# A band and time attention block: the feed-forward transposes behind the second product, the output products half a step later, the band scores of four heads in turn, a reciprocal on VectorE at the change to gelu

## The chip, the cores and the metric

The kernel runs on one core of one Trainium2 chip. The core has TensorE (PE, the matrix engine, with its weight loads shown apart as PEld), VectorE (DVE), ScalarE (ACT), GpSimd (POOL) and a queue for transfers (SP). Each engine executes its own instructions in order, and semaphores tie the engines together. The metric is the time of one execution in device microseconds (us); several runs are taken, and their median counts. A profile of one execution gives each instruction's start and duration.

## The reference

The input x has shape (2, 256, 128, 128): batch, time, band, channel. Three blocks follow each other, each added to x:

```python
xt = _ln(x, ln_t_w, ln_t_b).transpose(0, 2, 1, 3)
x = x + _mha(xt, t_wi, t_bi, t_wo, t_bo, H_T, cm).transpose(0, 2, 1, 3)
xf = _ln(x, ln_f_w, ln_f_b)
x = x + _mha(xf, f_wi, f_bi, f_wo, f_bo, H_F, bm)
xn = _ln(x, ln_n_w, ln_n_b)
h = jax.nn.gelu(xn @ w1.T + b1, approximate=False)
x = x + (h @ w2.T + b2)
```

The first attends over the 256 times of one band with a causal mask, the second over the 128 bands of one time with a mask that keeps bands at most 16 apart. Both have four heads of 32 channels; the softmax is over the keys. The third has 512 hidden channels. All of it is float32.

## The kernel before

**Groups.** `BoundedPath.groups` (L824) cuts the work into groups of four rows of 128 tokens. There are 128 groups of attention over time (`OverTime`, L599), whose results go to a buffer in HBM. Then come 32 batches of sixteen times each: a batch has four groups of attention over bands (`OverBands`, L673), called A0 to A3 here, and four groups of feed-forward (`FeedForward`, L736), called F0 to F3, that work on what A0 to A3 left in the tile `x2`. F0 needs what A0 wrote, F1 what A1 wrote, and so on.

**Order.** Every instruction of PE, DVE, ACT and POOL goes through `InOrder` (L786), which pins it in the order in which the program writes it. That order is written out by hand in `run` (L876). Its loop takes one step n for each group; in step n it issues pieces of several groups: `do(n, ...)` is a piece of group n, `do(n - 1, ...)` one of the group before. `near(n, far, name)` issues a preparing piece for a group further on, which is group n + 2 + far for attention and n + 1 + far for feed-forward (`AHEAD`, L430 and L737). So each engine has a queue that is fixed beforehand, and an instruction that waits holds up all that stand behind it on its engine.

**The pieces of a group of attention.**

- `statistics` (L444): mean and variance of four rows on DVE (bn_stats, bn_aggr), then 1/sqrt on POOL in two instructions (the tile `rstd`). `normalize` (L456): four instructions on DVE (`xh`). `transpose` (L465): four transposes on PE into one bank (`xp`). `take_transposed` (L472): a copy on DVE (`xnT`).
- `queries_keys`, `values`: the products `qp`, `kp`, `vp` on PE; their copies to SBUF (`qT`, `kT`, `v`) run on ACT, for time groups `kT` on DVE.
- `scores`: the products `sp`, keys by queries, one head in one quarter of PE's rows (32 of 128), each head in a bank of its own. `weights`: the exponentials on ACT (tiles `pt` for time, `pf` for bands), then the mask: selects on POOL, two for each band head, and for the fourth band head one multiplication with a 0/1 band on DVE. Band groups did heads 0 and 1 in `first_half` and `first_function`, heads 2 and 3 in `second_half` and `second_function`.
- `bias`: on POOL, the residual plus a constant row.
- `weigh`: the denominators `rp` (products with ones) and the weighted values `op`. `invert` (L563): on ACT the logarithm of `rp` and the exponential of its negative, a first estimate `r` of the reciprocal. `divide` (L571): on DVE one Newton step and the division, `t`, `u` and `oT`.
- `output` (L581): four products `yp` on PE. `finish` (L589): on DVE, `yp` added to the residual; time groups then issue two stores.

**The pieces of a feed-forward group.** `statistics` to `take_transposed` as above. `hidden` and `gelus`: four products `hp` on PE and four gelus `hT` on ACT, two in the first half, two in the second. `weigh`: the second product `zp`, 16 products. `divide`: on DVE, `zp` added to the residual `res`, and a store.

Each product in float32 appears as two instructions in the trace. All results of PE go through one set of eight PSUM banks (L807), which the tiles take in turn. ACT needs one table for exp and ln and another for gelu, so it changes its table twice in each batch: `preload_act_table_set` (L898) ahead of A0, and by itself ahead of F0's first gelu. In the step of F0 (`turn`) the exponentials of A3's reciprocal stand ahead of F0's gelus, so that the table changes after them.

Of the kernel before, what the change touches and what calls it, by code (L numbers as in the profile page):

```python
# [9 lines left out]
F32 = mybir.dt.float32  # L10
# [3 lines left out]
ALU = mybir.AluOpType  # L14
# [4 lines left out]
P = 128  # L19
H = 4  # L20
# [4 lines left out]
NT = 4  # L25
# [4 lines left out]
EXP_SET = "natural_log_exp_and_others"  # L30
# [393 lines left out]
class Group:  # L424
# [52 lines left out]
    def first_half(self):  # L477
        pass

    def first_function(self):  # L480
        pass

    def second_half(self):
        pass

    def second_function(self):
        pass
# [25 lines left out]
    def output(self):  # L513
        pass
# [5 lines left out]
class Attention(Group):  # L520
# [50 lines left out]
    def divide(self):  # L571
# [6 lines left out]
        self.oT = path.work.tile([P, NT * P], F32, name="oT", bufs=2)  # L578
        vector.scalar_tensor_tensor(self.oT, t, 2.0, u, ALU.subtract, ALU.mult)

    def output(self):  # L581
        path = self.path
        self.yp = path.bank([P, NT, P], "yp")
        for i in range(NT):
            path.tensor.matmul(
                self.yp[:, i], self.oT[:, i * P : (i + 1) * P], path.k.wn[self.which], start=True, stop=True
            )
# [85 lines left out]
class OverBands(Attention):  # L673
# [32 lines left out]

    def first_half(self):
        self.p = self.path.work.tile([P, H, NT, P], F32, name="pf", tag="p")
        self.scores((0, 1))

    def first_function(self):
        self.weights((0, 1))

    def second_half(self):
        self.scores((2, 3))

    def second_function(self):
        self.weights((2, 3))

    def weigh(self):  # L720
        path = self.path
# [79 lines left out]
class BoundedPath:  # L801
# [74 lines left out]
    def run(self, x, out):  # L876
        groups = list(self.groups(x, out))

        def do(n, *names):
            if 0 <= n < len(groups):  # L880
                for name in names:
                    getattr(groups[n], name)()

        def near(n, far, name):

            for d in (1, 2):
                if 0 <= n + d + far < len(groups) and groups[n + d + far].AHEAD == d:
                    do(n + d + far, name)

        def at(n, kind):  # L890
            return 0 <= n < len(groups) and isinstance(groups[n], kind)

        self.scalar.preload_act_table_set(EXP_SET)
        for n in range(-7, len(groups) + 2):

            turn = at(n, FeedForward) and at(n - 1, OverBands)
            if at(n, OverBands) and at(n - 1, FeedForward):
                self.scalar.preload_act_table_set(EXP_SET)  # L898
            do(n + 7, "load")
            near(n, 1, "statistics")  # L900
            near(n, 0, "normalize")
            do(n, "first_half")
            if not turn:
                do(n, "first_function")
            do(n, "bias")
            do(n - 1, "weigh", "invert", "divide")
            if turn:
                do(n, "first_function")
            do(n, "second_half", "second_function")
            do(n + 1, "queries_keys", "take_query", "take_key", "values", "take_values")  # L910
            near(n, 0, "transpose")
            near(n, 0, "take_transposed")
            do(n - 1, "output", "finish")


def bounded_path(tc, k, x, out):
# [66 lines left out]
```

## Time and profile before

| what | value |
|---|---|
| median of 3 runs | 3305.75 us (3305.04 to 3305.8) |
| profiled execution, its own time | 3304.75 us |
| its span | 3302.9 us |
| granted clock of TensorE | 0.999 |
| PE busy | 3183.9 us (96%) |
| DVE busy | 2191.5 us (66%) |
| POOL busy | 1843.4 us (56%) |
| ACT busy | 1803.8 us (55%) |
| stretch 100 to 1000 us (time groups): PE busy | 900 of 900 us |
| stretch 1600 to 3000 us (batches): PE busy | 1338.5 of 1400 us |

Busy time is the time in which an engine executes at least one instruction. The ends of PE's instructions are modelled, and its instructions overlap, so its busy share is not the share of its peak; what a piece costs is better read as the distance from its start to the start of what follows. The list of groups gives, for one kind of instruction, its count, its busy time, its mean duration in ns, and the idle time of its engine just before it with what ended that time. The view of waits sums that idle time by who waited for whom: total, number, longest.

### The profile page before, as it was taken

Reading aid. Unit: us, or ns where it says so; the run is one execution under the profiler, and the core shown is the slowest. Engines: PE = TensorE matmul, PEld = TensorE weight load, DVE = VectorE, ACT = ScalarE, POOL = GpSimd, SP = SyncE. Lnnn points to the kernel's source line nnn. Section 1 sums busy time; section 2 is a strip of 40 time slices with the busy share of each in tenths; the row PEclk is TensorE's granted clock in tenths of the full one; section 3 lists DMA queues with packets and bytes.
Section 4 is the critical chain, followed back from the end, with each engine's and each line's share of the span. In section 5 each row is a group of like instructions: output and inputs, shape, how many; then the busy total and the mean of one; then the engine's idle time right before and its main releaser. Section 6 shows DMA issues by size and latency. Waiting matters only on the chain.

```text
span 3302.9 us, 77870 instructions
## 1 busy us (share of the span) xinstructions
PE 3183.9 (96%) x31270; PEld 2259.0 (68%) x31270; DVE 2191.5 (66%) x6446; ACT 1803.8 (55%) x3264; POOL 1843.4 (56%) x2441
## 2 busy tenths in 40 slices
PE   7999999999999999999999999999999999999998
PEld 5666666666666766676667666676667666677666
DVE  6777777777777766566665666566665666566664
ACT  4666666666666654555445544555445545455544
POOL 4555555555555655456555565455555565455554
PEclk9999999999999999999999999999999999999999
DMA  3222222222222111110111011110111011110000
GB/s 80 59 70 57 72 56 59 72 56 72 56 59 72 52 40 30 33 30 27 39 33 33 27 39 30 33 30 27 39 33 33 27 37 32 33 30 27 27 20 21
DMA packets 222866, 140.57 MB, mean 43 GB/s; under 512 B 7968, under 2 KB 205984, under 8 KB 222496
## 3 DMA queue, kind: packets, MB, share of 16 engines
q1 hardware_dynamic: 221248, 134.45, 14.5%
q8 instruction: 249, 4.08, 0.5%
q10 hardware_dynamic: 1248, 1.05, 0.1%
q14 instruction: 121, 0.99, 0.1%
HBM read 68.36 MB, written 67.11 MB: 41 GB/s over the span
## 4 chain that ended last, share of the span: by engine, by line
PE 89%; DVE 7%; ACT 2%; issue 1%; DMA 0%; POOL 0%; SPq 0%; ACTq 0%; DVEq 0%
PE sp L796 14%; PE zp L796 14%; PE hp L796 12%; PE rp L796 10%; PE qp L796 8%; PE vp L796 7%; PE op L796 7%; PE kp L796 7%; PE yp L796 6%; PE xp L796 4%; DVE xnT L796 2%; DVE oT L796 1%; DVE t L796 1%; ACT r L796 1%; DVE u L796 1%; ACT ln L796 1%
## 5 line engine op out<-in xcount | busy, mean ns | idle before, releaser
L796 POOL TENSOR_SCALAR rstd<-mv 128x4 f32<-128x4 f32 x384 | 88.1, 229 | 1225.5 <-DVE mv L796 1223.8
L796 ACT ACTIVATE hT<-hp,b 128x512 f32<-128x512 f32 x512 | 341.3, 687 | 514.4 <-PE hp L796 510.6
L796 POOL TENSOR_SCALAR_AFFINE_SELECT pf<-pf 128x512 f32<-128x512 f32 x768 | 545.3, 718 | 100.3 <-ACT pf L796 74.1
L796 ACT ACTIVATE pt<-sp 128x384 f32<-128x384 f32 x1024 | 419.3, 496 | 303.5 <-PE sp L796 303.5
L796 PE MATMUL hp<-xnT,w1f 128*128 128x512 f32 x1024 | 493.9, 605 | 52.9 <-DVE xnT L796 52.9
L796 PE MATMUL sp<-qT,kT 32*128 32x128 f32 (+1 forms) x8192 | 536.2, 315 | 0.0
L796 PEld LDWEIGHTS zp<-w2T_sb,hT 128*128 128x128 f32 x4096 | 475.0, 192 | 50.4 <-issue 46.4
L796 PEld LDWEIGHTS sp<-qT,kT 32*128 32x128 f32 x8192 | 433.2, 185 | 87.6 <-issue 55.1
L796 DVE COPY xnT<-xp 128x512 f32<-128x512 f32 x384 | 261.8, 689 | 333.2 <-PE xp L796 332.0
L796 PE MATMUL zp<-w2T_sb,hT 128*128 128x128 f32 x4096 | 481.5, 276 | 0.1
L796 ACT ACTIVATE pf<-sp 128x512 f32<-128x512 f32 x512 | 277.9, 595 | 306.1 <-PE sp L796 282.9
L796 POOL TENSOR_TENSOR rstd<-rstd,mhalf 128x4 f32<-128x4 f32 x384 | 405.0, 1055 | 32.0
L796 DVE TENSOR_TENSOR t<-rp,r 128x512 f32<-128x512 f32 x256 | 177.0, 692 | 314.3 <-ACT r L796 311.8
L796 PEld LDWEIGHTS vp<-wf,xnT 128*128 128x128 f32 x2048 | 269.7, 192 | 123.0 <-issue 92.2
L796 POOL TENSOR_SCALAR_AFFINE_SELECT pt<-pt 128x512 f32<-128x512 f32 x512 | 314.0, 637 | 58.5 <-ACT pt L796 58.4
L796 PE MATMUL yp<-wn,oT 128*128 128x128 f32 x2048 | 275.1, 277 | 43.1 <-DVE oT L796 43.1
L796 PEld LDWEIGHTS hp<-xnT,w1f 128*128 128x128 f32 x1024 | 174.2, 190 | 202.0 <-issue 131.3
L796 PEld LDWEIGHTS yp<-wn,oT 128*128 128x128 f32 x2048 | 248.6, 192 | 56.4 <-PE xp L796 56.4
L796 PE MATMUL qp<-xnT,wf 128*128 128x512 f32 x512 | 285.8, 640 | 0.8 <-DVE xnT L796 0.8
L796 DVE SCALAR_TENSOR_TENSOR oT<-t,u 128x512 f32<-128x512 f32 x256 | 272.9, 1066 | 8.9
L796 PE MATMUL vp<-wf,xnT 128*128 128x128 f32 x2048 | 270.5, 275 | 0.0
L796 DVE TENSOR_TENSOR res<-zp,res 128x512 f32<-128x512 f32 x128 | 88.5, 691 | 268.4 <-issue 142.0
(92 smaller groups left out, 4730.2 us busy)
## 6 DMA issues: line engine op xcount, KB each, us to landing
xt<-in_x SPq DMA_DIRECT2D x64, 512.0 KB, 5.5
x<-rd SPq DMA_DIRECT2D x256, 128.0 KB, 2.1
out<-res SPq DMA_DIRECT2D x128, 256.0 KB, 2.3
xb<-x SPq DMA_DIRECT2D x32, 0.5 KB, 6.1
w1T_sb<-in_w1T ACTq DMA_DIRECT2D x1, 256.0 KB, 4.0
w2T_sb<-in_w2T ACTq DMA_DIRECT2D x1, 256.0 KB, 4.3
t_wiT_sb<-in_t_wiT ACTq DMA_DIRECT2D x1, 192.0 KB, 2.5
f_wiT_sb<-in_f_wiT ACTq DMA_DIRECT2D x1, 192.0 KB, 3.8
```

The lines of the kernel that those rows point to most:

```text
L796: return self.tc.keep_in_program_order(emit(*args, **kwargs))
```

## The change

1. Band groups issue the scores of all four heads at once, block by block with four heads in turn, then four exponentials and all the selects. `second_half` and `second_function` of band groups are gone.
2. `output` and `finish` of a group move from the end of the next step to the step after it: in most steps right behind `normalize`, ahead of the scores. In the step of F0 they stand behind F0's four hidden products and gelus, in that of F1 behind `zp` and the transposes. `statistics`, which stood ahead of `normalize`, now stand behind `finish`.
3. The transposes and their copy for feed-forward groups (and, in the step of F2, for A0 of the next batch) move from the end of the step to a place behind the second product `zp` and ahead of the second pair of hidden products. F0's stand in the step of A3 behind the scores, F1's in the step of F0 behind `output` of A2.
4. In the step of F0 all four hidden products and gelus are issued first, then A3's `rp` and `op`. A3's reciprocal is taken by `divide_alone`: one DVE reciprocal of `rp` and one multiplication, with neither ACT nor the Newton step.

```diff
+    def divide_alone(self):
+
+        path, vector = self.path, self.path.vector
+        r = path.work.tile([P, NT * P], F32, name="r", bufs=2)
+        vector.reciprocal(r, self.rp)
+        self.oT = path.work.tile([P, NT * P], F32, name="oT", bufs=2)
+        vector.scalar_tensor_tensor(self.oT, self.op, -1.0, r, ALU.mult, ALU.mult)
...
     def first_half(self):
         self.p = self.path.work.tile([P, H, NT, P], F32, name="pf", tag="p")
-        self.scores((0, 1))
+        self.scores(range(H))
 
     def first_function(self):
-        self.weights((0, 1))
-
-    def second_half(self):
-        self.scores((2, 3))
-
-    def second_function(self):
-        self.weights((2, 3))
+        self.weights(range(H))
...
+        def move(n):
+            near(n, 0, "transpose")
+            near(n, 0, "take_transposed")
+
         self.scalar.preload_act_table_set(EXP_SET)
         for n in range(-7, len(groups) + 2):
-
-            turn = at(n, FeedForward) and at(n - 1, OverBands)
-            if at(n, OverBands) and at(n - 1, FeedForward):
-                self.scalar.preload_act_table_set(EXP_SET)
+            feeding = [at(n - i, FeedForward) for i in range(3)]
             do(n + 7, "load")
-            near(n, 1, "statistics")
             near(n, 0, "normalize")
-            do(n, "first_half")
-            if not turn:
-                do(n, "first_function")
-            do(n, "bias")
-            do(n - 1, "weigh", "invert", "divide")
-            if turn:
-                do(n, "first_function")
-            do(n, "second_half", "second_function")
-            do(n + 1, "queries_keys", "take_query", "take_key", "values", "take_values")
-            near(n, 0, "transpose")
-            near(n, 0, "take_transposed")
-            do(n - 1, "output", "finish")
+            if feeding[0] and at(n - 1, OverBands):
+
+                do(n, "first_half", "first_function", "second_half", "second_function")
+                do(n - 2, "output", "finish")
+                near(n, 1, "statistics")
+                move(n)
+                do(n, "bias")
+                do(n - 1, "weigh", "divide_alone")
+            elif feeding[1] and at(n - 2, OverBands):
+                do(n, "first_half", "first_function", "bias")
+                do(n - 1, "weigh", "divide")
+                move(n)
+                do(n - 2, "output", "finish")
+                near(n, 1, "statistics")
+                do(n, "second_half", "second_function")
+            else:
+                do(n - 2, "output", "finish")
+                near(n, 1, "statistics")
+                if feeding[1] and at(n, OverBands):
+                    self.scalar.preload_act_table_set(EXP_SET)
+                do(n, "first_half", "first_function", "bias")
+                early = at(n, OverBands) and at(n + 1, FeedForward)
+                if early:
+                    move(n)
+                do(n - 1, "weigh", "invert", "divide")
+                if feeding[0] and at(n + 1, FeedForward):
+                    move(n)
+                    early = True
+                do(n, "second_half", "second_function")
+                do(n + 1, "queries_keys", "take_query", "take_key", "values", "take_values")
+                if not early:
+                    move(n)
```

## The prediction

> **What bounds the kernel now.** I read the page's chain of waits first, then who waits for whom, then the order of time of TensorE (PE) over one batch of four band groups A0 to A3 and four feed-forward groups F0 to F3.
>
> ```profile
> PE 89%; DVE 7%; ACT 2%; issue 1%; DMA 0%; POOL 0%; SPq 0%; ACTq 0%; DVEq 0%
> ```
>
> PE makes up 89% of the chain. What PE executes, and the few places where it stands still, set the end. The view of waits:
>
> ```profile
> PE hp L796 <- DVE xnT L796: 52.9, 96, 0.8
> PE yp L796 <- DVE oT L796: 43.1, 64, 1.0
> ```
>
> 96 and 64 waits are three and two in each of the 32 batches, so all of PE's real idle time lies in the second part of the program; the time groups have none. In the next four fences (start, duration, engine, operation, count, then the idle time before in brackets) the distance from one start to the next is what a piece costs PE, because a matmul's modelled end overlaps its successor.
>
> ```profile
> 1499.98 1.13 PE L796 MATMUL yp<-wn,oT 128*128 128x128 f32 x8 [0.97 <-DVE oT L796]
> ```
>
> ```profile
> 1510.86 3.73 PE L796 MATMUL zp<-w2T_sb,hT 128*128 128x128 f32 x32
> 1514.43 1.88 PE L796 MATMUL hp<-xnT,w1f 128*128 128x512 f32 x4
> 1516.14 0.60 PE L796 MATMUL xp<-ident,xh 128*128 128x128 f32 x4
> 1517.53 1.98 PE L796 MATMUL hp<-xnT,w1f 128*128 128x512 f32 x4 [0.78 <-DVE xnT L796]
> ```
>
> ```profile
> 1544.93 0.60 PE L796 MATMUL xp<-ident,xh 128*128 128x128 f32 x4
> 1545.46 1.16 PE L796 MATMUL sp<-qT,kT 32*128 32x128 f32 x16
> 1546.55 1.06 PE L796 MATMUL rp<-pf,ones 128*32 128x512 f32 x8
> 1547.43 1.06 PE L796 MATMUL op<-pf,v 128*32 128x128 f32 x32
> 1548.42 1.16 PE L796 MATMUL sp<-qT,kT 32*128 32x128 f32 x16
> 1549.51 1.12 PE L796 MATMUL qp<-xnT,wf 128*128 128x512 f32 x2
> 1550.47 1.02 PE L796 MATMUL kp<-xnT,wf 128*128 128x512 f32 x2
> 1551.33 1.05 PE L796 MATMUL vp<-wf,xnT 128*128 128x128 f32 x8
> 1552.22 0.60 PE L796 MATMUL xp<-ident,xh 128*128 128x128 f32 x4
> 1552.66 1.06 PE L796 MATMUL yp<-wn,oT 128*128 128x128 f32 x8
> 1553.64 1.16 PE L796 MATMUL sp<-qT,kT 32*128 32x128 f32 x16
> ```
>
> ```profile
> 1567.67 1.13 PE L796 MATMUL yp<-wn,oT 128*128 128x128 f32 x8 [0.97 <-DVE oT L796]
> ```
>
> From the first of these rows to the last is one batch: 1567.67 - 1499.98 = 67.69 us. The prices that I use, each a distance of two starts: one set of band scores of two heads 1.09 (1545.46 to 1546.55), denominators rp 0.88, weighted values op 0.99, qp 0.96 (0.86 where no other tile shape stands before it, like kp), kp 0.86, vp 0.89, one transpose xp 0.44 (0.53 where scores follow, 1544.93 to 1545.46), output yp 0.98 before scores (0.89 elsewhere, being eight instructions of vp's shape), second product zp 3.57, a pair of hidden products hp 1.72. The row of 1517.53 shows a removable stall: hp stood 0.78 us for xnT, because the transposes run just ahead of it, and after the stall it took 1.98 where the row of 1514.43 took 1.88, so 0.1 us more is lost on restarting.
>
> **Scores of four heads in turn.** A set is 16 instructions for two heads; the change issues one set of 32 for four. Time groups already run four heads:
>
> ```profile
> 503.06 0.94 PE L796 MATMUL sp<-qT,kT 32*128 32x256 f32 x16
> 503.93 1.50 PE L796 MATMUL rp<-pt,ones 128*32 128x512 f32 x16
> ```
>
> There each head streams 2 x (256 + 128) = 768 columns in 503.93 - 503.06 = 0.87 us, 1.13 ns a column; in the band set each head streams 2 x 4 x 128 = 1024 columns in 1.09 us, 1.06 ns a column. The time follows one head's columns, no matter whether two or four heads are at work. So four heads should take 1.09 us, and each band group loses one set: 4 x 1.09 = 4.36 us a batch. Bounds for the new set are 1.09 and 2.18; I take 1.09, the nearer by the time-group row.
>
> **What the other engines do with it.** The exponentials now come four in a row on ScalarE (ACT), ahead of the logarithm of the group before, which used to stand after two.
>
> ```profile
> 1546.70 1.08 ACT L796 ACTIVATE pf<-sp 128x512 f32<-128x512 f32 x2 [0.98 <-PE sp L796]
> 1547.76 0.60 ACT L796 ACTIVATE ln<-rp 128x512 f32<-128x512 f32 x1
> 1548.39 0.63 ACT L796 ACTIVATE r<-ln 128x512 f32<-128x512 f32 x1
> ```
>
> Exponentials start 1546.70 - 1545.46 = 1.24 us after the scores' first matmul, 1.08/2 = 0.54 each; ln 0.63 from start to start; r 0.63. Next, VectorE (DVE) during one band step:
>
> ```profile
> 1551.70 1.11 DVE L796 TENSOR_TENSOR pf<-pf,band 128x512 f32<-128x512 f32 x1
> 1552.86 0.69 DVE L796 COPY xnT<-xp 128x512 f32<-128x512 f32 x1
> 1553.82 0.69 DVE L796 TENSOR_TENSOR x<-yp,x 128x512 f32<-128x512 f32 x1 [0.27 <-PE yp L796]
> 1554.55 0.87 DVE L796 BATCH_NORM_STATS2 stats<-x 128x6 f32<-128x128 f32 x4
> 1555.34 0.36 DVE L796 BATCH_NORM_AGGREGATE mv<-stats 128x2 f32<-128x6 f32 x4
> 1557.23 0.69 DVE L796 TENSOR_TENSOR t<-rp,r 128x512 f32<-128x512 f32 x1 [1.54 <-ACT r L796]
> 1557.84 0.68 DVE L796 TENSOR_TENSOR u<-op,r 128x512 f32<-128x512 f32 x1
> 1558.56 1.02 DVE L796 SCALAR_TENSOR_TENSOR oT<-t,u 128x512 f32<-128x512 f32 x1
> ```
>
> Now each place where PE could have to wait, with 0.1 us for the hand-over from DVE to PE (an estimate: finish, in the row of 1553.82, begins 1.16 after yp's start, and yp's modelled length in the row of 1552.66 is 1.06).
>
> *yp of A0 and A1.* From the scores' start of the next group: 1.24 + 4 x 0.54 + ln 0.63 + r 0.63 + t, u, oT 2.35 (1557.23 to 1558.56 + 1.02) + 0.1 = 7.11 us. PE meanwhile has, for A0, sp 1.09 + rp 0.88 + op 0.99 + qp 0.96 + kp 0.86 + vp 0.89 + xp 0.44 = 6.11, and for A1 the same without xp, 5.67. PE waits 1.00 and 1.44. Before, the second score set stood in this stretch and ln came after two exponentials, so the row of 1552.66 shows no wait: **part of the gain is given back here.** Moving output into the next step changes nothing on PE, since it stood last in its step and now stands first.
>
> *hp of F0.* The copy xnT of F0 stands in DVE's queue behind the band mask of A3's fourth head: 1.24 + 2.16 + mask 1.11 + copy 0.69 + 0.1 = 5.30 us after A3's scores start; PE has sp 1.09 + xp 0.53 + rp 0.88 + op 0.99 = 3.49. Wait 1.81 us. Queued behind that mask too are t, u and oT of A2; they end about 2.4 us after the copy, under F0's four hidden products (2 x 1.72 = 3.44), so yp of A2, now behind those, waits for nothing.
>
> *hp of F1.* After yp of A2 starts, DVE runs finish (1.16 later), statistics to 1555.34 + 0.36, that is 1.88 from finish's start, then copy 0.69, + 0.1: 3.83 us. PE has yp 0.89 + xp 0.53 + rp 0.88 + op 0.99 = 3.29. Wait 0.54 us.
>
> *F2, F3.* Transposes now stand behind zp and ahead of a pair of hidden products, which need nothing new and last 1.72 us; the copies (0.69 each) lie beneath them. The stall of 1517.53 and its sisters go. If that cover were gone they would be back at 0.78 us apiece.
>
> *The selects on GpSimd (POOL).* Three groups of instructions (name, count, busy time, mean ns of one), and the pieces of a normalization on DVE:
>
> ```profile
> L796 POOL TENSOR_SCALAR_AFFINE_SELECT pf<-pf 128x512 f32<-128x512 f32 x768 | 545.3, 718 | 100.3 <-ACT pf L796 74.1
> ```
>
> ```profile
> L796 POOL TENSOR_TENSOR rstd<-rstd,mhalf 128x4 f32<-128x4 f32 x384 | 405.0, 1055 | 32.0
> ```
>
> ```profile
> L796 POOL TENSOR_SCALAR rstd<-mv 128x4 f32<-128x4 f32 x384 | 88.1, 229 | 1225.5 <-DVE mv L796 1223.8
> ```
>
> ```profile
> L796 DVE TENSOR_SCALAR xh<-x,mv,rstd 128x128 f32<-128x128 f32 x512 | 140.5, 338 | 0.0
> ```
>
> Six selects a group at 0.718, now in one run: 4.3 us, from the first exponential's end, 1.78 after the scores' start. The tight place is A0, whose statistics now stand behind four xh (4 x 140.5/512 = 1.1 us) on DVE, and whose selects stand behind the two rstd instructions on POOL: copy 0.1 + 0.69, xh 1.1, statistics 1.15 (1554.55 to 1555.34 + 0.36), rstd 0.23 + 1.06 end about 4.4 after A0's scores start, the selects at 8.7; rp comes at 7.80 + 1.09 = 8.9 (7.80 is A0's length in the sum below). I put 0.2 us there.
>
> *Time groups.* Normalization moves ahead of finish and statistics; both come four xh, 1.1 us, later.
>
> ```profile
> DVE t L796 <- ACT r L796: 311.8, 254, 1.8
> ```
>
> DVE stands idle before t for 311.8/254 = 1.2 us on average, which takes this in. On POOL the two rstd instructions come later by as much, and the selects of a time group by no more:
>
> ```profile
> 509.32 1.22 POOL L796 TENSOR_SCALAR_AFFINE_SELECT pt<-pt 128x512 f32<-128x512 f32 x2 [0.46 <-ACT pt L796]
> ```
>
> ```profile
> 512.52 1.50 PE L796 MATMUL rp<-pt,ones 128*32 128x512 f32 x16
> ```
>
> The selects end at 509.32 + 1.22 = 510.54, and the rp that reads them starts at 512.52: 2.0 us to spare. The pairs of stores on the SP queue that finish issues go out 1.1 us later, for loads that come many steps on; rd has five buffers and three are alive. I cost all of this at nothing. PSUM's eight banks go round; each use eight allocations on finds its last reader done, the four score banks of a band step included, which four exponentials empty in 4 x 0.54 = 2.2 us.
>
> *Reciprocal on DVE.* At F0, ln, exp, t and u of A3 go, and one reciprocal from PSUM plus oT come, once a batch. No row shows it. It starts when F1's xnT copy ends, 0.1 before F1's hidden products; next come oT 1.02 and normalization of F2 1.1; the transposes of F2 stand 1.72 + 0.1 + 3.57 = 5.4 later on PE. So a reciprocal of up to 5.4 + 0.1 - 1.02 - 1.1 = 3.4 us is hidden, and each us above costs 1 us a batch, 32 us. From below the nearest row is t (0.69, same shape, same PSUM operand); as the slow end I take the whole of ln, r, t, u that it replaces, 0.63 + 0.63 + 0.61 + 0.72 = 2.6. Both are hidden; I take no cost. The Trainium skill, VectorE: DVE Perf Modes, says under "Walkthrough: the 8-slice pipeline in each mode" that a reciprocal is an iterative divide with a repeat count of 8, and gives DVE's clock as 0.96 GHz under "Specifications"; by an estimate from these two, 8 x 512 / 0.96 = 4.3 us, the sum would come out 0.9 us a batch or 29 us higher. No run here shows it yet.
>
> **The sum.** PE from A0's scores to the next A0's, without waits: A0 1.09 + 3.57 + 0.86 + 0.86 + 0.89 + 0.53 = 7.80; A1 6.11; A2 5.67 + 0.98 = 6.65; A3 0.98 + 3.49 = 4.47; F0 3.44 + 3.29 = 6.73; F1 3.44 + 3.57 + 0.44 + 0.89 = 8.34; F2 3.44 + 3.57 + 0.88 = 7.89; F3 3.44 + 3.57 + 0.86 + 0.86 + 0.89 + 0.53 = 10.15. Total 58.14. New waits 1.00 + 1.44 + 1.81 + 0.54 + 0.2 = 4.99, four restarts 0.4, and 0.25 for two or three changes of tile shape that these distances leave out (0.1 each, as qp shows): 63.8 us. The gain is 67.69 - 63.8 = 3.9 us a batch, x 32 = 125 us. The profiled execution took 3304.75 us (span 3302.9 and 1.85 around it), so 3180; it lies 1.0 under the median of the runs shown, which at this size changes nothing.
>
> **Rivals.**
> 1. The forecast, 3180. Its own ends: oT shorter than 1.02 by 0.33 (as short as t) at both yp, 2 x 0.33 x 32 = 21 less; as much longer, and A0's selects later by 0.4, 34 more: 3159 to 3214. Chance 0.50.
> 2. The reciprocal outlasts its cover by about a us: it goes over its elements six or seven times where t (0.69) goes once, 4.1 to 4.8 us, against 3.4 of cover. F2's transposes wait on PE for the normalization behind it: 0.7 to 1.4 us a batch, 3180 + 1.0 x 32 = 3212. No row speaks for or against it, so it gets about half the forecast's chance, 0.27. (The Trainium skill's page named above would have it here, at 3209.)
> 3. The change does not do what it says: four heads in turn take 2.18 us. Then PE has 4.36 more, the waits of yp shrink by 1.0 and 1.1, and that before F0 stays: + 2.2 a batch, 3180 + 71 = 3251. The time groups' row speaks against it. Chance 0.06.
> 4. The waits of PE that I count don't come, because DVE and ACT run ahead of the times I gave: 5.4 x 32 = 173 less, 3007. The chains above are made of rows in series, so chance 0.04.
> 5. Slower: the reciprocal again, now so long that DVE at F1 is the bound. From 3.4 + 3.9 = 7.3 us, ten times the row of t, it eats the gain; at 8.5 the kernel takes 3180 + 5.1 x 32 = 3343. Against it: ACT, which computes the same function as ln and r, takes 0.63 for each pass over the same 512 elements. Chance 0.08.
> 6. Between: a reciprocal near that point, no change, 0.05.
>
> Faster by over 0.2% (6.6 us, about what a measurement of this kernel can tell from no change): 0.50 + 0.27 + 0.06 + 0.04 = 0.87; within 0.05; slower 0.08. The range takes in cases 1 to 3: 3145 to 3255, and leaves out 0.17.
>
> **What would show it.** Period of a batch near 63.8 us. Score sets of 32 instructions with 1.09 us to rp: right; 2.2: rival 3. Waits of PE for oT twice a batch, one to one and a half us each, and for xnT before F0 and F1; none at F2 and F3. A row of the reciprocal under 3.4 us with no wait of xp for xh in F1: right; longer with such a wait: rivals 2 or 5. Waits of rp for the selects, in either stage, or any idle time of PE among the time groups, would prove me wrong about POOL and about DVE's new order.

## The result, and the profile after

| what | before | after |
|---|---|---|
| median of 4 runs each | 3305.39 us | 3131.2 us (3130.63 to 3132.49) |
| ratio, with its 95% interval | | 0.9474 (0.9457 to 0.949) |
| profiled execution, its span | 3302.9 us | 3128.7 us |
| granted clock of TensorE | 0.999 | 0.999 |
| PE busy | 3183.9 us | 3013.3 us |
| DVE busy | 2191.5 us | 2246.7 us |
| ACT busy | 1803.8 us | 1748.6 us |
| POOL busy | 1843.4 us | 1889.3 us |

The change gains 174 us. The prediction had 125, and 3131 lies 14 us below the lower end of its range. The chain of waits after:

```profile
PE 80%; DVE 13%; ACT 5%; issue 1%; DMA 0%; POOL 0%; SPq 0%; ACTq 0%; POOLq 0%; DVEq 0%
```

PE's share of the chain falls from 89% to 80%, and DVE's rises from 7% to 13%: more of the end is now set by DVE finishing something for PE. The view of PE's waits (total, number, longest):

```profile
PE yp L798 <- DVE oT L798: 46.8, 64, 0.9
PE hp L798 <- DVE xnT L798: 34.0, 64, 0.8
PE xp L798 <- DVE xh L798: 20.5, 33, 10.7
```

64 and 64 are two and two in each batch. hp waited three times a batch before; its stalls at F2 and F3 are gone, and those at F0 and F1 are here, as forecast. Of the 33 waits for `xh`, one of 10.7 us is the program's start, as before (10.5); the other 32, 9.8 us together, are new, one in each batch, and the prediction did not have them. Adding up, PE's idle time in a batch is (46.8 + 34.0 + 9.8) / 32 = 2.83 us against (52.9 + 43.1) / 32 = 3.00 before. So the idle time hardly fell: the gain is work and small losses that PE no longer has. PE in order of time (start, duration, engine, operation, count, idle before):

```profile
1504.95 1.17 PE L798 MATMUL sp<-qT,kT 32*128 32x128 f32 x32
...
1512.87 1.17 PE L798 MATMUL sp<-qT,kT 32*128 32x128 f32 x32
...
1519.80 1.13 PE L798 MATMUL yp<-wn,oT 128*128 128x128 f32 x8 [0.65 <-DVE oT L798]
1520.86 1.17 PE L798 MATMUL sp<-qT,kT 32*128 32x128 f32 x32
1521.96 1.07 PE L798 MATMUL rp<-pf,ones 128*32 128x512 f32 x8
...
1527.51 1.13 PE L798 MATMUL yp<-wn,oT 128*128 128x128 f32 x8 [0.80 <-DVE oT L798]
1528.57 1.17 PE L798 MATMUL sp<-qT,kT 32*128 32x128 f32 x32
...
1530.52 0.33 PE L798 MATMUL xp<-ident,xh 128*128 128x128 f32 x1 [0.30 <-DVE xh L798]
...
1533.48 3.70 PE L798 MATMUL hp<-xnT,w1f 128*128 128x512 f32 x8 [0.76 <-DVE xnT L798]
1537.02 1.05 PE L798 MATMUL yp<-wn,oT 128*128 128x128 f32 x8
...
1540.71 1.96 PE L798 MATMUL hp<-xnT,w1f 128*128 128x512 f32 x4 [0.31 <-DVE xnT L798]
...
1567.14 1.17 PE L798 MATMUL sp<-qT,kT 32*128 32x128 f32 x32
```

One batch runs from 1504.95 to 1567.14, 62.19 us; before it took 67.69. 31 distances from batch to batch make 31 x 5.5 = 170 of the 174 us. The time groups gained and lost nothing, but for the first of them: there `rp` waits 1.5 us for the selects, once, where it waited 0.5 before. The prediction had none.

With each start-to-start distance put down to the tile that it begins with, and idle time taken out, the 5.5 us of a batch are these: scores 8.72 before, 4.40 after, 4.32 less; weighted values 0.41 less, hidden products 0.29 less, `yp` 0.17 less, the others 0.15 less together, which I put down to losses around a stall or a change of tile shape; idle time 0.16 less. **By this account the set of four heads is four fifths of the gain**; what it needs of the new order for that, the experiments show. It takes 1520.86 to 1521.96 = 1.10 us with 32 instructions, where 16 took 1.09.

DVE in the same batch:

```profile
1526.67 0.69 DVE L798 SCALAR_TENSOR_TENSOR oT<-t,u 128x512 f32<-128x512 f32 x1
1527.28 3.18 DVE L798 TENSOR_SCALAR xh<-x,mv,rstd 128x128 f32<-128x128 f32 x4
...
1531.88 0.36 DVE L798 BATCH_NORM_AGGREGATE mv<-stats 128x2 f32<-128x6 f32 x4
1532.16 0.66 DVE L798 TENSOR_TENSOR pf<-pf,band 128x512 f32<-128x512 f32 x1
1532.74 0.68 DVE L798 COPY xnT<-xp 128x512 f32<-128x512 f32 x1
...
1540.48 3.34 DVE L798 RECIPROCAL r<-rp 128x512 f32<-128x512 f32 x1
```

and ACT:

```profile
1522.10 2.06 ACT L798 ACTIVATE pf<-sp 128x512 f32<-128x512 f32 x4 [2.76 <-PE sp L798]
1524.03 0.63 ACT L798 ACTIVATE ln<-rp 128x512 f32<-128x512 f32 x1
```

Three things differ from the forecast here. oT of 1526.67 takes 0.69 us (forecast 1.02), the mask of 1532.16 takes 0.66 and its successor starts 0.58 after it (forecast 1.11), and four `xh` take 3.18 us at 1527.28 (forecast 1.1). On ACT, four exponentials in a row take 1524.03 - 1522.10 = 1.93, 0.48 each (forecast 0.54). The reciprocal takes 3.34 us. The groups of one batch (count, busy time, mean ns), first before:

```profile
L796 DVE TENSOR_TENSOR pf<-pf,band 128x512 f32<-128x512 f32 x5 | 5.6, 1110 | 1.5 <-ACT pf L796 1.5
...
L796 DVE TENSOR_SCALAR xh<-x,mv,rstd 128x128 f32<-128x128 f32 x16 | 4.3, 335 | 0.0
...
L796 DVE SCALAR_TENSOR_TENSOR oT<-t,u 128x512 f32<-128x512 f32 x4 | 3.8, 954 | 0.1
```

then after:

```profile
L798 DVE TENSOR_SCALAR xh<-x,mv,rstd 128x128 f32<-128x128 f32 x16 | 7.9, 558 | 0.4 <-POOL rstd L798 0.4
...
L798 DVE TENSOR_TENSOR pf<-pf,band 128x512 f32<-128x512 f32 x4 | 3.2, 791 | 2.7 <-ACT pf L798 2.7
...
L798 DVE SCALAR_TENSOR_TENSOR oT<-t,u 128x512 f32<-128x512 f32 x3 | 2.4, 787 | 0.1
```

The kind and the shape of each instruction are the same on both sides, and the lengths are not. What sets them is asked in the experiments below.

### The profile page after: what moved, and what is told of

Read it like the earlier page. It is cut to its first block, busy times and chain, and to the rows that moved or that the text cites. A ratio compares the mean times of both kernels' runs of the same rounds, so it can differ in the third digit from the quotient of the medians.

```text
span 3128.7 us, 77496 instructions
## 1 busy us (share of the span) xinstructions
PE 3013.3 (96%) x31270; PEld 2133.5 (68%) x31270; DVE 2246.7 (72%) x6414; ACT 1748.6 (56%) x3200; POOL 1889.3 (60%) x2441
## 4 chain that ended last, share of the span: by engine, by line
PE 80%; DVE 13%; ACT 5%; issue 1%; DMA 0%; POOL 0%; SPq 0%; ACTq 0%; POOLq 0%; DVEq 0%
PE zp L798 15%; PE hp L798 15%; PE sp L798 10%; PE yp L798 7%; PE rp L798 7%; PE qp L798 6%; PE op L798 6%; PE vp L798 5%; PE kp L798 5%; PE xp L798 4%; DVE xh L798 3%; ACT pf L798 3%; DVE stats L798 2%; DVE oT L798 2%; DVE t L798 1%; DVE x L798 1%
## 5 line engine op out<-in xcount | busy, mean ns | idle before, releaser
L798 POOL TENSOR_SCALAR rstd<-mv 128x4 f32<-128x4 f32 x384 | 99.2, 258 | 1131.9 <-DVE mv L798 1131.9
L798 ACT ACTIVATE hT<-hp,b 128x512 f32<-128x512 f32 x512 | 351.9, 687 | 620.8 <-PE hp L798 616.4
L798 POOL TENSOR_SCALAR_AFFINE_SELECT pf<-pf 128x512 f32<-128x512 f32 x768 | 533.9, 711 | 38.6 <-ACT pf L798 12.3
L798 PE MATMUL hp<-xnT,w1f 128*128 128x512 f32 x1024 | 471.5, 598 | 34.0 <-DVE xnT L798 34.0
L798 PE MATMUL sp<-qT,kT 32*128 32x128 f32 (+1 forms) x8192 | 389.4, 315 | 0.0
L798 ACT ACTIVATE pf<-sp 128x512 f32<-128x512 f32 x512 | 264.4, 602 | 202.9 <-PE sp L798 202.6
L798 PEld LDWEIGHTS sp<-qT,kT 32*128 32x128 f32 x8192 | 310.8, 185 | 64.6 <-issue 35.9
L798 PE MATMUL yp<-wn,oT 128*128 128x128 f32 x2048 | 275.1, 277 | 46.8 <-DVE oT L798 46.8
L798 DVE TENSOR_TENSOR t<-rp,r 128x512 f32<-128x512 f32 x224 | 154.5, 690 | 174.8 <-ACT r L798 173.9
L798 DVE TENSOR_SCALAR xh<-x,mv,rstd 128x128 f32<-128x128 f32 x512 | 256.3, 562 | 15.1 <-POOL rstd L798 15.1
L798 PE MATMUL kp<-xnT,wf 128*128 128x512 f32 x512 | 262.3, 594 | 0.0
```

What stands on the lines that cost most here:

```text
L798: return self.tc.keep_in_program_order(emit(*args, **kwargs))
```

## The experiments

The theory: 1.09 us saved for each band group, the stalls at F2 and F3 gone, and four waits of PE that give part of it back, whose size follows from what DVE does between a group's scores and the tile that PE waits for. The rivals: the reciprocal is exposed; the scores or the order alone carry the gain; the lengths of mask and oT are their own and PE's waits are set by something else.

### Scores of four heads alone

On the kernel before:

```diff
     def first_half(self):
...
-        self.scores((0, 1))
+        self.scores(range(H))
     def first_function(self):
-        self.weights((0, 1))
-
-    def second_half(self):
-        self.scores((2, 3))
-
-    def second_function(self):
-        self.weights((2, 3))
+        self.weights(range(H))
```

> Four heads in turn alone, everything else in the order of before. Theory (the scores' gain is given back as waits for VectorE unless the order is changed with it): PE saves 4.36 us a batch and 0.2 for a change of tile shape fewer, and the 0.6 us that rp of A2 stood for the selects; new or longer waits are 0.9 at yp of A0, 1.2 at yp of A1 and 2.1 more at yp of A2, which stands only 3.5 us behind A3's scores; hp of F0 waits 0.4 less. Net 1.4 us a batch, 43 us: 3262 us. Rival (the scores pay in full wherever they stand): 4.56 x 32 = 146 us less, 3159 us.

Measured: 3274.4 us, ratio 0.9909 (0.9881 to 0.9938). That is 30 us of gain, and 12 short of the expectation's 3262. PE in order of time:

```profile
1559.46 1.13 PE L790 MATMUL yp<-wn,oT 128*128 128x128 f32 x8 [3.02 <-DVE oT L790]
1560.42 3.56 PE L790 MATMUL hp<-xnT,w1f 128*128 128x512 f32 x4
```

and the window of those four hidden products (PE, PEld, DVE, ACT and POOL busy, then the granted clock of PE and the share and rate of transfers):

```profile
1560.42:1563.83 3.41, 3.41 (x6) 0.96 (x4) 2.85 (x13) 0.00 (x0) 2.95 (x4) 0.51 0.02 5
```

`yp` of A2 still stands ahead of the first hidden products in F0's neighbourhood, with too little work between the scores and it, and waits 3.02 us. After that idle time PE's granted clock is 0.51 for 3.41 us, and a pair of hidden products takes 3.56 us, where the same four instructions took 1.98 in the row of 1517.53 before. The wait of 3.02 us stands in every batch, the lower clock behind it in about every other (65.76 and 67.4 us in turn). The mean clock is 0.990; (0.999 - 0.990) x 3273 = 29 us went that way. PE's idle time in a batch rises by (153.9 + 36.6) / 32 - 3.00 = 2.95 us (waits of `yp` for oT and of hp for `xnT`, by the view of waits). So of some 4.4 us saved in a batch, three turn into waits and nearly one into lost clock.

### The new order alone

On the kernel after, scores in two pairs again:

```diff
     def first_half(self):
...
-        self.scores(range(H))
+        self.scores((0, 1))
     def first_function(self):
-        self.weights(range(H))
+        self.weights((0, 1))
+
+    def second_half(self):
+        self.scores((2, 3))
+
+    def second_function(self):
+        self.weights((2, 3))
```

> The changed kernel with the band scores again in two sets of two heads. Theory: PE has 4.56 us a batch more, but its waits at yp of A0 (0.81), yp of A1 (0.98) and hp of F0 (1.42), measured in the changed kernel, go, since ln and the mask no longer stand behind four exponentials: 1.35 a batch, 43 us more than the changed kernel, 3174 us. Rival (scores and order simply add up): 146 us more, 3277 us.

Measured: 3228.23 us, 0.977 (0.9741 to 0.9798): 76 us of gain, where I expected 130. I missed a wait. PE between F0's and F1's hidden products:

```profile
1553.05 3.70 PE L804 MATMUL hp<-xnT,w1f 128*128 128x512 f32 x8
...
1558.36 0.33 PE L804 MATMUL xp<-ident,xh 128*128 128x128 f32 x1 [0.25 <-DVE xh L804]
1559.07 0.33 PE L804 MATMUL xp<-ident,xh 128*128 128x128 f32 x1 [0.38 <-DVE xh L804]
...
1561.52 1.95 PE L804 MATMUL hp<-xnT,w1f 128*128 128x512 f32 x4 [0.25 <-DVE xnT L804]
```

With two pairs, the normalization of F1 stands behind the mask of A3's second pair and runs while POOL does its selects; the four `xh` take 3.19 us, and the transposes wait for them one by one:

```profile
1555.82 3.19 DVE L804 TENSOR_SCALAR xh<-x,mv,rstd 128x128 f32<-128x128 f32 x4
```

F0's to F1's hidden products take 1561.52 - 1553.05 = 8.47 us against 1540.71 - 1533.48 = 7.23 in the kernel after; over 32 batches that is 40 of the 54 us that I missed, and the rest stays open. Scores alone 30, order alone 76, both 174: 68 us come only with both. The rows of the two runs suggest why: the order supplies the work that covers what the single set uncovers, and the single set brings the mask and the normalization forward.

### A second reciprocal

```diff
+        twice = path.work.tile([P, NT * P], F32, name="twice", bufs=1)
+        vector.reciprocal(twice, self.rp)
         vector.reciprocal(r, self.rp)
```

> The changed kernel with a second DVE reciprocal of the same bank ahead of the one that is used. Theory (a cover of 3.4 us that one reciprocal of 3.35 just fills, with 0.35 us left by the trace): 3.35 - 0.35 = 3.0 us a batch on PE, at the transposes of F2, 96 us: 3227 us. Rival (VectorE has more room there than the trace shows, because what is behind it is needed later): within 10 us of 3131.

Measured: 3215.64 us, 0.9732 (0.9703 to 0.976). A batch takes 64.77, 2.57 more than the kernel after, and PE waits where it should:

```profile
1564.86 1.10 PE L800 MATMUL xp<-ident,xh 128*128 128x128 f32 x4 [1.91 <-DVE xh L800]
```

So a reciprocal of 3.35 us leaves 3.35 - 2.57 = 0.78 us of cover. The prediction had the cover at 3.4, just enough; it is 4.1. Of the difference, 0.4 is oT, which I took at 1.02 us and behind which `xh` starts after 0.61 in the kernel after (1543.93 to 1544.54); the rest comes mainly from the transposes, which need the four rows of `xh` one after the other and not all at the start. The reciprocal of the change costs PE nothing.

### The old reciprocal at F0

```diff
-                do(n - 1, "weigh", "divide_alone")
+                do(n - 1, "weigh")
+                self.scalar.preload_act_table_set(EXP_SET)
+                do(n - 1, "invert", "divide")
```

> The changed kernel with A3's reciprocal taken on ScalarE again (ln, exp and the Newton step), behind F0's gelus, with one more change of the table before it and one after. Theory (VectorE's reciprocal lies under F1's first hidden products and zp, and so would ScalarE's): by the rows of the changed kernel ln could start 1.6 us after the last gelu, oT would end about 1.5 us earlier than with the reciprocal, and F1's first gelu would come 0.3 us later; PE waits for neither: 3131 us within 6. Rival (the reciprocal is part of the gain): two table loads of 1.28 us a batch come to the time, 82 us, 3213 us.

Measured: 3129.92 us, 0.9471 (0.9452 to 0.949), the same as the kernel after. With two table changes more on ACT, the logarithm and exponential are hidden in that place too. So the reciprocal on DVE is worth nothing by itself in this place; what the place is worth was not measured alone.

### Output back at the end of the step

Statistics first again, and `output` and `finish` last, but for A2 and A3:

```diff
             do(n + 7, "load")
+            usual = not (feeding[0] and at(n - 1, OverBands) or feeding[1] and at(n - 2, OverBands))
+            if usual:
+                near(n, 1, "statistics")
...
             else:
-                do(n - 2, "output", "finish")
-                near(n, 1, "statistics")
...
+                if not at(n + 1, FeedForward):
+                    do(n - 1, "output", "finish")
```

> The changed kernel with statistics ahead of normalization and with output and finish at the end of the step again, except for A2 and A3, whose outputs stay behind the hidden products. Theory (the move matters at one place alone, F0's normalization, which now waits behind finish of A1 and the statistics of F1): xp of F0 waits about 2 us, of which hp of F0 already stood for 1.4, so 0.6 a batch more, 19 us: 3150 us; nothing changes among the time groups. Rival (the move costs or gains nothing): 3131 us.

Measured: 3143.56 us, 0.9513 (0.9486 to 0.9541); a batch takes 0.41 us more, and no wait appears among the time groups. The move of `output`, with `finish` and the statistics, is worth 12 us. "Moving output changes nothing on PE" was nearly right; what it moves is DVE's order, and the waits of `xp` for `xh` grow from 20.5 to 49.5 us.

### The band mask twice

```diff
                 path.vector.tensor_tensor(blk, blk, path.band.unsqueeze(1).to_broadcast([P, NT, P]), ALU.mult)
+                path.vector.tensor_tensor(blk, blk, path.band.unsqueeze(1).to_broadcast([P, NT, P]), ALU.mult)
```

> The changed kernel with the 0/1 mask of the fourth band head multiplied in twice, so that VectorE is busy 0.69 us more in front of t and of the copy for F0. It stands for what I had priced too high: mask 1.11 and oT 1.02, against 0.69 each in most places of the changed kernel. Theory (those lengths lie one to one on PE's path at yp of A0, yp of A1 and hp of F0): 0.69 at yp of A0, 0.23 at yp of A1 (where t otherwise waits 0.46 for ScalarE), 0.69 at hp of F0: 1.6 us a batch, 51 us: 3182 us. Rival (the difference to the forecast came from elsewhere, and these lengths are hidden): 3131 us.

Measured: 3292.03 us, 0.9952 (0.9924 to 0.998), far above both expectations; its four runs lie between 3275 and 3301. PE around `yp` of A0:

```profile
1552.14 1.13 PE L799 MATMUL yp<-wn,oT 128*128 128x128 f32 x8 [2.39 <-DVE oT L799]
1553.20 1.94 PE L799 MATMUL sp<-qT,kT 32*128 32x128 f32 x32
1555.07 1.91 PE L799 MATMUL rp<-pf,ones 128*32 128x512 f32 x8
```

and the window of those scores and denominators (columns as above):

```profile
1553.20:1556.78 3.58, 3.58 (x42) 2.04 (x45) 1.84 (x9) 1.60 (x4) 1.36 (x3) 0.53 0.00 0
```

Two effects add up. After 2.39 us of idle time the granted clock is 0.53, and scores take 1.87 us instead of 1.10; the mean clock of 0.981 is (0.999 - 0.981) x 3291.5 = 59 us. And batches without such a stretch take 65.31, that is 3.1 us more than the kernel after, 100 us in all: in one of them (`yp` of A0 at 1353.31) `yp` of A0 waits 2.39 us, 1.7 longer, `yp` of A1 1.69, 0.9 longer, and hp of F0 1.59, 0.8 longer. That is more than one mask each. On DVE at A0, in the batch of the rows above, the four `xh` ahead of the masks take 3.20 us where they took 1.99, the two masks take 1.71 us, and the oT behind them takes 1.74 where it took 0.98. So this run shows that time of DVE in these places is passed on to PE, but not one to one, since more of DVE now meets the selects. The kernel after stands near an edge: half a us to a us more on DVE in these places costs far more than itself.

### The selects taken away

On the kernel after and on the kernel before, the selects on POOL are left out, so that heads 0 to 2 of the band groups are unmasked:

```diff
-            for s in (1, -1):
-                path.gpsimd.affine_select(
-                    out=blk, in_=blk, compare_op=ALU.is_ge, fill=path.zero, base=BAND,
-                    pattern=[[0, NT], [-s, P]], channel_multiplier=s,
-                )
```

> The changed kernel without the selects of the band groups on POOL, so heads 0 to 2 stay without their band mask there. Theory (VectorE's mask, oT and xh last longer wherever one of POOL's instructions is under way, and each of them waits for it to end): all of mask and oT at about 0.69 us, all of xh at 0.34, where the changed kernel has means of 0.79, 0.74 and 0.56. On PE's path that is 0.3 us a batch at yp of A0 and 0.1 at hp of F0; xp of F0 no longer waits: 3118 us. Rival (these lengths have to do with the engine's own order or with what ScalarE writes): lengths and time as in the changed kernel, 3131 us.

> The kernel before without the selects of the band groups on POOL, so heads 0 to 2 stay without their band mask there. Theory (the 1.11 us of the mask and the 1.02 of oT that the forecast was worked out from hold POOL's selects in them): both at about 0.69 us. The time falls by the 0.6 us a batch that rp of A2 waits for the selects, 19 us: 3286 us. Rival (mask and oT are that long by themselves in this order): 1.1 and 1.0 as before.

Measured: 3109.77 us, 0.9409 (0.939 to 0.9427), and 3272.73 us, 0.9902 (0.9882 to 0.9921): 21 us below the kernel after and 33 below the kernel before, where I expected 13 and 19. (On the kernel before, the waits of hp for `xnT` fell too, from 52.9 to 36.6 us, which I had not counted.) The groups of one batch of the kernel after without selects:

```profile
L793 DVE TENSOR_TENSOR pf<-pf,band 128x512 f32<-128x512 f32 x4 | 2.8, 692 | 4.8 <-ACT pf L793 4.8
...
L793 DVE SCALAR_TENSOR_TENSOR oT<-t,u 128x512 f32<-128x512 f32 x3 | 2.1, 692 | 0.1
```

and of the kernel before without them:

```profile
L791 DVE SCALAR_TENSOR_TENSOR oT<-t,u 128x512 f32<-128x512 f32 x4 | 2.8, 692 | 0.1
...
L791 DVE TENSOR_TENSOR pf<-pf,band 128x512 f32<-128x512 f32 x4 | 2.7, 686 | 1.5 <-ACT pf L791 1.5
```

The mask takes 0.69 us on both sides and oT 0.69 on both. (The kernel after without selects still has waits of `yp`, 33.2 us in all, put down by the view of waits to the copy of v on ACT. At `yp` of A1 that copy ends at 1522.62 + 0.58 = 1523.20 and oT at 1522.50 + 0.69 = 1523.19, so the view cannot tell which of them holds it, and no run here parts them.) **Their longer times were never their own: they ran against POOL's instructions, the selects and the bias that stands behind them.** Before, the mask averaged 1.11 and oT 0.95 in a batch; after, 0.79 and 0.79. The same goes for the four `xh` of F0: 1.11 us without selects, and 3.18 in the row of 1527.28, where the last of them lies under the bias (1529.11, 1.27 us). Single instructions of POOL in the batch of after that is shown above tell how (the second is the second half of an `rstd`, the fifth the first half of another):

```profile
1518.48 0.64 POOL L798 TENSOR_SCALAR_AFFINE_SELECT pf<-pf 128x512 f32<-128x512 f32 x1
1523.31 1.04 POOL L798 TENSOR_TENSOR rstd<-rstd,mhalf 128x4 f32<-128x4 f32 x1
1526.04 0.64 POOL L798 TENSOR_SCALAR_AFFINE_SELECT pf<-pf 128x512 f32<-128x512 f32 x1
1526.75 1.11 POOL L798 TENSOR_SCALAR_AFFINE_SELECT pf<-pf 128x512 f32<-128x512 f32 x1
1532.34 0.57 POOL L798 TENSOR_SCALAR rstd<-mv 128x4 f32<-128x4 f32 x1 [1.96 <-DVE mv L798]
```

The oT of A0, on DVE, is this one:

```profile
1518.68 0.98 DVE L798 SCALAR_TENSOR_TENSOR oT<-t,u 128x512 f32<-128x512 f32 x1
```

It begins at 1518.68 in the middle of the select of 1518.48, and takes 0.98 us. The oT of 1526.67 begins just as one select ends (1526.04 + 0.64 = 1526.68) and ahead of the next (1526.75), and takes 0.69; now that next select takes 1.11 where the others take 0.64. The mask of 1532.16 finds POOL idle and takes 0.66; `rstd`, begun under it, takes 0.57, where its mean in the run is 0.26. **In these rows, whoever begins first runs at its own length and the other waits.** Not every instruction of POOL takes part: the second half of an `rstd` runs from 1523.31 to 1524.35, and the mask that begins under it at 1524.20 takes 0.69 us. On the side of before, the oT of 1558.56, whose 1.02 us went into the prediction, began in the middle of this select:

```profile
1558.40 0.64 POOL L796 TENSOR_SCALAR_AFFINE_SELECT pf<-pf 128x512 f32<-128x512 f32 x1
```

The mask of 1551.70, whose 1.11 us went into it too, began in the middle of a select as well (1551.18, 1.09 us). What reads an operand from PSUM (t, u, the copies) takes 0.66 to 0.69 in the rows of before and of after, with selects beside it or without. That a DVE instruction with two operands in SBUF and a POOL instruction keep each other out agrees with the Trainium skill, "SBUF — State Buffer", section "🔬 SBUF: two separate sides", where DVE and GpSimd share a pair of ports as an exclusive lock, which whoever starts first holds for its whole instruction. The rows show the waiting, in both directions, 0.98 us for 0.69 and 1.11 for 0.64, and the one exception above; the ports themselves no row shows.

### The logarithm between the exponentials

An attempt at a faster version: in every band group ln and r stand between the second and third exponential, and the mask behind oT.

```diff
     def first_function(self):
-        self.weights(range(H))
+        self.weights((0, 1))
+
+    def second_function(self):
+        self.weights((2, 3))
...
-                do(n - 1, "weigh", "invert", "divide")
+                do(n - 1, "weigh", "invert")
+                if bands:
+                    do(n, "second_function", "bias")
+                do(n - 1, "divide")
+                if bands:
+                    do(n, "mask_last")
```

> The changed kernel with ln and r of the group before put between the second and the third exponential of a band group, and the mask of the fourth head behind oT. Theory (yp's waits are the two extra exponentials and the mask ahead of t): the waits at yp of A0 and A1 go (0.81 + 0.98, and 0.1 each for restarting), hp of F0 comes 0.5 us earlier, the exponentials that come 1.26 us later reach their selects in time: 2.4 us a batch, 77 us less than the changed kernel: 3054 us. Rival (POOL, with its selects starting late, or the later exponentials become what rp waits for): 3100 us or more.

Measured: 3185.2 us, 0.9636 (0.962 to 0.9652): slower than the kernel after by 54. The wait of `yp` of A0 is gone and that of A1 is 0.33 us, but PE pays elsewhere:

```profile
1541.52 0.58 PE L805 MATMUL xp<-ident,xh 128*128 128x128 f32 x2 [0.86 <-DVE xh L805]
...
1550.98 0.33 PE L805 MATMUL xp<-ident,xh 128*128 128x128 f32 x1 [0.91 <-DVE xh L805]
```

`xh` of F0 and F1 now run wholly among selects and the bias, and the transposes wait for them row by row. A batch takes 63.0 or, with a stretch of lower clock, 64.35 us; the mean clock is 0.988, about 35 us. No single wait here is longer than 0.91 us: the lower clock from 1487.80 stands behind three of them at F1's transposes, 0.20, 0.37 and 0.90.

### Waits taken away one by one

The last attempt keeps the logarithm between the exponentials for A1's step alone, with the mask behind oT, and in A3's step puts the copy for F0 ahead of F1's statistics and of the mask:

```diff
                 if early:
+                    g = groups[n]
                     move(n)
+                    near(n, 1, "moments")
+                    g.exponentials(range(H))
+                    g.masks((0, 1))
+                    near(n, 1, "deviation")
+                    g.masks((2, 3))
+                    do(n, "bias")
+                    do(n - 1, "weigh", "invert", "divide")
+                elif second:
...
+                    g.exponentials((0, 1))
+                    g.masks((0, 1))
+                    do(n - 1, "weigh", "invert")
+                    g.exponentials((2, 3))
+                    g.masks((2,))
+                    do(n, "bias")
+                    do(n - 1, "divide")
+                    g.masks((3,))
```

> The changed kernel with two pieces moved. In A3's step the copy for F0 stands ahead of the statistics of F1 and of the mask, and on POOL the two instructions of F1's deviation stand between the selects of head 1 and head 2. In A1's step alone ln and r of A0 stand between the second and the third exponential, and A1's mask behind oT of A0. Theory (hp of F0 stands for the copy that is queued behind the mask; yp of A0 for two exponentials too many; both free of POOL's selects): hp of F0 comes 1.1 us earlier, yp of A0 0.8 us, and 0.1 each for restarting: 2.1 a batch, 67 us less than the changed kernel: 3064 us. Rival (the selects get in the way of xh of F1 as they did when ln was moved in all band groups, and PE's clock falls in stretches of many short waits): no better than 3120 us.

Measured: 3107.62 us, 0.9401 (0.9386 to 0.9417), the fastest of all: 24 us below the kernel after, with no work left out. PE around F0 and F1:

```profile
1523.95 1.17 PE L809 MATMUL sp<-qT,kT 32*128 32x128 f32 x32
...
1528.04 3.70 PE L809 MATMUL hp<-xnT,w1f 128*128 128x512 f32 x8
...
1533.27 0.84 PE L809 MATMUL xp<-ident,xh 128*128 128x128 f32 x3 [0.49 <-DVE xh L809]
...
1536.23 1.96 PE L809 MATMUL hp<-xnT,w1f 128*128 128x512 f32 x4 [0.26 <-DVE xnT L809]
```

The wait of `yp` of A0 is gone (0.8 us a batch), and hp of F0 follows the scores after 4.09 us without a wait, against 4.91. But 0.96 of it comes back before F1 (8.19 against 7.23). The mask now stands behind the copy, and ahead of F1's normalization it and oT meet POOL: the mask takes 1.00 us at 1528.03 and oT 1.13 at 1530.27, so `xh` of F1, `finish` of A2 and the copy for F1 come later behind hp of F0. That is the main reason why 24 us came and not the 67 that I expected.

## Why the prediction was right and where it was wrong

**What bounds it, the saved sets, the moved transposes.** Right. PE sets the end, a set of 32 takes 1.10 us (forecast 1.09), the stalls at F2 and F3 are gone, the time groups are unchanged but for one wait at their start, and the selects are early enough for every `rp` of a batch (forecast 0.2 us at A0, measured none). For A3 only just: its selects, now in one run of 4.41 us from 1534.01, end at 1538.42, and its `rp` begins at 1538.44. The two half experiments show that neither edit does it alone.

**The reciprocal.** Right that it is hidden, for the cover of 3.4 us that I gave, and by luck in its size: 3.35 us is above the rows that bounded it (0.69 to 2.6). The cover was larger than I said, 4.1. Rival 2 had the place where a longer one would show, at F2's transposes, but too great a length for it. The estimate of 4.3 us worked out from the Trainium skill, "VectorE: DVE Perf Modes", is not borne out: the row has 3.34. The second reciprocal shows what a reciprocal twice as long would have cost: 84 us.

**The failed step: the new waits of PE.** Each was forecast in its place, and each was forecast too long. Start to start, less what PE has to do (the sum is more than the 2.83 us of idle time above, which the view counts from modelled ends):

| wait | forecast | measured | from |
|---|---|---|---|
| `yp` of A0 | 1.00 | 0.81 | 1519.80 - 1512.87 - 6.12 |
| `yp` of A1 | 1.44 | 0.98 | 1527.51 - 1520.86 - 5.67 |
| hp of F0 | 1.81 | 1.42 | 1533.48 - 1528.57 - 3.49 |
| hp of F1 | 0.54 | 0.40 | 1540.71 - 1537.02 - 3.29 |
| `rp` of A0, for selects | 0.20 | 0 | no wait in the view |
| sum | 4.99 | 3.61 | |

The difference is 1.38 us a batch, and 0.2 more came from restarts and changes of tile shape, for which I had put 0.65 and which took 62.19 - 58.14 - 3.61 = 0.44: 1.6 x 32 = 51 us, the 49 that the forecast was off. The mis-sized terms are these. The mask, taken at 1.11 us from the row of 1551.70, cost 0.58 at F0. oT, taken at 1.02 from 1558.56, cost 0.69 at A1 (0.98 at A0). The exponentials, taken at 0.54 each from two of them, cost 0.48 in a run of four, so ln came 3.17 us after the scores instead of 3.40; that is the whole of the difference at A0. At F0 this was partly undone: the mask did not start behind the exponentials, but behind F1's statistics, which end at 1531.88 + 0.36, because the slow `xh` of 1527.28 had pushed all of DVE back. The same `xh` made the fourth transpose wait 0.30 us, inside the wait of hp. At F1 hp came 3.69 us behind `yp`, where the rows in series made 3.83.

The step that failed is the choice of durations, not the chain: 4.99 us of new waits a batch were forecast, 3.61 came. The row of oT was taken where it had begun in the middle of a select, and that of the mask in the same way (1.11 us, against 0.69 without selects); at F0 the mask began while POOL was idle, at A1 oT began in the gap between two selects. My range let oT shrink at two places, 21 us, and left mask and exponentials fixed, so its lower end came too high. For the mask the profile before had no short row to take, since the five of its batch average 1.11; oT, of the same shape, had both lengths there, 0.69 (1499.15) and 1.02, and could have warned me. The selects left out of both kernels show that POOL is the cause of the lengths; that the shorter lengths are the cause of the shorter waits follows from the rows in series, and the doubled mask shows the reverse, DVE's time in those places passed on to PE, with the selects' share mixed in.

**Rivals.** Four heads in 2.18 us: refuted by the row of 1520.86. No waits at all: refuted by the view of waits. Slower by a reciprocal of 7.3 us: refuted by its row.

## What to carry to other kernels

When a step moves to another place, take the duration of its instructions from rows with the same neighbours on the other engines, or keep both lengths for the range: here 0.69 or 1.11 us for the same mask, by whether POOL was in the middle of a select when it began. Where PE works at its full clock and waits for a us, count what one us more of wait could do to the clock before spending it: the doubled mask lost about 59 us that way. And test two edits apart: the set of four heads brought 30 us alone, the order 76, both together 174.

## What the runs showed of the hardware

- Behind waits of PE its granted clock can fall to a half for 3.41 us, and the length of one wait does not decide alone. It fell behind 2.39 us (mask twice, clock 0.53 in the window) and 3.02 us (scores alone, 0.51, in about every other batch that has this wait). With two reciprocals, where a wait of 1.91 us stands in nearly every batch, it fell in two of 32 (0.50 from 1175.07 and from 2147.87; the mean clock stayed at 0.999), and with the logarithm between behind 0.20, 0.37 and 0.90 us close together (0.50 from 1487.80). Those two stretches begin 2147.87 - 1175.07 = 972.80 us apart, 285 times 3.413, so where a wait falls may count beside its length; no run here tests that.
- A reciprocal on DVE of 128x512 float32 from PSUM takes 3.35 us, five times a multiplication of that shape, 0.69.
- DVE and POOL hold each other up, instruction by instruction: 0.69 or 0.98 us for the same oT, and 0.64 or 1.11 us for the same select, in one batch. The second half of an `rstd` on POOL is an exception: a mask begun under it took 0.69.
